# Linear attention with a top-2 MoE FFN on one core: TensorE takes the tile loop in source order instead of the planner's

## The chip, the cores and the metric

The kernel runs on one core of a Trainium2 chip. The metric is the device time of that core in microseconds (us), as the median of several runs.

## The reference

The input x has 8 sequences of 1024 tokens with 256 features, all in float32. In short:

```python
xn = layernorm(x)
# linear attention, 16 heads of 16
q, k, v = xn @ Wq.T, xn @ Wk.T, xn @ Wv.T
q, k = elu(q) + 1, elu(k) + 1
kv = cumsum over tokens of (k outer v)        # per head, causal
den = clip(q . cumsum(k), 1e-6)
att = (q . kv / den) @ Wo.T
# mixture of experts: 8 experts, two per token
logits = xn @ Wr + br
weights, experts = top_k(logits, 2); weights = softmax(weights)
y_e = (silu(xn @ W1[e]) * (xn @ W3[e])) @ W2[e]     # 256 -> 512 -> 256
out = x + att + sum over the token's two experts of weight * y_e
```

## The kernel before

**Tiling.** The 8192 tokens are cut into 16 blocks of 512 (`NBLK`); a block has 4 chunks of 128. The MoE part works on tiles of 128 rows that belong to one expert. The rows of a tile are gathered by an indirect DMA, and its weights are fetched by expert number. 132 such tiles are run by the loop, and up to three more behind it under a condition. The first 25 tiles come from a first list that covers the first 2048 tokens only, so that the loop can begin while the other 12 blocks are still to be normalised and routed. The other tiles come from a second list over the rest.

**Prelude.** The first four blocks are normalised and routed, and the first list is built, in an order written by hand (`tc.manual_schedule` for VectorE, ScalarE, TensorE and GpSimd). It is not changed.

**The tile loop** is `for j in range(NM + 1)`. One iteration holds, in the source, these parts:

- `ffn_norm(j + 1)` (ScalarE) normalises the gathered rows of the next tile. Up to tile 26 they are transposed on TensorE (`ffn_turn`, tile `xg_t`); from tile 27 on by a DMA on 16-bit halves (`ffn_halves`, `ffn_turn_halves`, joined by `ffn_join`).
- For j = 1 to 11 one token block t = 4 + j is prepared. `moments` works out mean and variance of two blocks at once on VectorE (at even j): for each of 8 chunks a `bn_stats` and a `bn_aggr` (L282, L283), then a reciprocal square root by Newton steps. `normalise(t)` is four ScalarE activations (L317). `turn(t)` is eight transposes on TensorE (L332, tile `tp`) with a ScalarE copy for each half (`xnT`, L337). `logits` is eight matmuls of 32 columns (L355), copied to `lgT`, turned once more (`lg_t`, L376) and added to `lg_all` on VectorE by `add_logits`. After every fourth block `route` picks the two experts on VectorE; its first part runs up to some counts, and the rest, driven by exhausting the generator `routing`, begins with the count matmuls on TensorE (`cnt_ps`, L442 and L448, read at L453).
- At j = 12 (`LISTS`) `second_batch` begins to build the second list, and one `next(lists)` per tile for j = 12 to 21 drives it. It has 32 groups of four matmuls (`held_ps`, L724) of one-hot matrices that VectorE makes for each group (`at_place` L572, `held` L585, `parts` L590); ScalarE makes the other half of `parts` with four multiplications (L592). In between, VectorE counts other tokens and works out `fills`.
- For j = 12 to 23 a DMA copies a piece of x into the output.
- `attend_upto(n)` moves the attention on. It has 9 steps a block: projections to q, k and v (`zq` L794; `zkk`, `zkv` L810; eight matmuls each), transposes, denominators, and one step for each chunk. A chunk's step issues on TensorE: `attend` of the chunk before it (`a_ps`, L990, 2 matmuls with `oT`), `carry` (`o_ps<-qT,kv`, L930), `scores` of the next chunk (`s_ps`, L911, eight matmuls of 32 rows), `weigh` (`o_ps<-s_sb`, L948, 16 matmuls of 32 columns, and L958, eight for the new `kv`). VectorE applies four causal masks to the scores (`s_sb`, L918), and makes `oT` (L965) and `kv` (L968, L977).
- `ffn_step(j)` starts the DMAs of later tiles and issues `ffn_hidden(j)`: gate and up, eight matmuls each (`gu_ps`, L1265), ScalarE's silu (L1273) and VectorE's product (`hT`, L1276). Then come `ffn_turn` or `ffn_join` of tile j + 1, and `ffn_out(j - 1)`: four matmuls (`y_ps`, L1284), scaled on VectorE (`y`, L1291), added to the output by an indirect DMA (L1295).

**What sets the order.** In the loop a planner orders the instructions of every engine; it reads the source as a list with dependencies and takes from what is ready by its own estimates. Only instructions inside `in_order(...)` keep the source's order among themselves. Each engine then takes its own list strictly in order. So the order on TensorE before is not that of the source: the transposes and logits of a block, for example, lie between single matmuls of the attention or of gate and up. When two attention steps fall into one iteration (this happens seven times from tile 26 on), the second step's `a_ps`, `carry` and `weigh` come between gate and up of the following tile.

**Buffers in PSUM.** `ps_mm` has four buffers (`gu_ps`, `s_ps`, `zq` and `zk`, `zv`), `ps_y` two (`y_ps`, `a_ps`, `lg_ps`, `lg_t`, `cnt_ps`, `held_ps`, the denominators), `ps_t` two (`tp`, `xg_t`, `o_ps`). A matmul waits until its buffer's last reader, on VectorE or ScalarE, is done.

Of the kernel before, what the change touches and what calls it, by code (L numbers as in the profile page):

```python
# [46 lines left out]
F32 = mybir.dt.float32  # L47
# [7 lines left out]
P = 128  # L55
# [9 lines left out]
def tile_attention_moe(  # L65
# [257 lines left out]
    def turn(t):  # L323
        xn = scaled.pop(t)
        if 0 < t < FB:
            xnT = e_one.tile([P, KC, TB], F32, name=f"xnT{t}")
        else:
            xnT = (two if t == 0 else f_two).tile([P, KC, TB], F32, tag="xnT", name="xnT")
        for k in range(KC):
            tp = ps_t.tile([P, TB], F32, tag="t", name="tp")  # L330
            for c in range(NCH):
                done = nc.tensor.transpose(  # L332
                    tp[:, bass.ts(c, P)], xn[:, c, bass.ts(k, P)], ident
                )
                if t == FB + 1:
                    in_order(done)
            nc.scalar.copy(xnT[:, k, :], tp)  # L337
        turned[t] = xnT
        if t == 0:
            turned_first.append(xnT)  # L340
        elif t != FB - 1:
            store(t)
# [352 lines left out]
    def second_batch(taken):  # L695

        rows = sizes(True)
        left = f_one.tile([P, E], F32, name="left")
        nc.vector.tensor_tensor(left, rows, taken, ALU.subtract)
        upto = add_up(left, "upto2")  # L700
        past = past_experts(upto, N2, f_x, "xb")
        te, te_i = numbers_of(past, N2, "2")
        nc.vector.tensor_copy(rows_left, upto[0:1, E - 1 : E])

        room = f_one.tile([P, E - 1], F32, name="room2")
        nc.vector.tensor_scalar(
            room, rows[:, 0 : E - 1], -1.0, float(ROWS), ALU.mult, ALU.add
        )
        nc.vector.tensor_tensor(room, room, taken[:, 1:E], ALU.add)
        of_tiles = rows_of(past, past, room, taken[:, 0:1], N2, "rows2")  # L710
        in_row, place = places(NT)

        short = f_one.tile([P, E], F32, name="short")
        nc.vector.tensor_scalar(short, rows, 1.5, None, ALU.is_lt)
        num_i = const.tile([P, N2], I32, name="of2_i")
        all_held = f_one.tile([P, N2], F32, name="all_held")
        yield
        for j in range(2):
            for a in range(0, NT, 16):
                ps = ps_y.tile([P, 2, N2], F32, tag="y", name="held_ps")  # L720
                for b in range(a, a + 16, PART):
                    at, parts = one_hot(in_row, place, of_tiles, j, b, N2)
                    for i in range(PART):
                        nc.tensor.matmul(  # L724
                            ps.rearrange("p w n -> p (w n)"), lhsT=at[:, i, :],
                            rhs=parts[:, i].rearrange("p w n -> p (w n)"),
                            start=(b + i == a), stop=(b + i == a + 15),
                        )
                for w in range(2):
                    if j == 0 and a == 0 and w == 0:  # L730
                        nc.vector.tensor_copy(all_held, ps[:, 0, :])
                    else:
                        nc.vector.tensor_tensor(all_held, ps[:, w, :], all_held, ALU.add)
                if j == 0 and a == 16:
                    fill = other_tokens(short)
                    fills = f_one.tile([P, N2], F32, name="fills")
                    for e in range(E):
                        mine = fills
                        if e > 0:
                            mine = f_two.tile([P, N2], F32, tag="mine", name="mine")  # L740
                        nc.vector.tensor_scalar(
                            mine, te, float(e), fill[:, e : e + 1], ALU.is_equal, ALU.mult
                        )
                        if e > 0:
                            nc.vector.tensor_tensor(fills, fills, mine, ALU.add)
                yield
        nc.vector.tensor_copy(num_i, all_held)
        _, src_i = tokens(all_held, N2, NT, "2_i")
        empty = f_one.tile([P, N2], F32, tag="at_i", name="empty")
        nc.vector.tensor_scalar(empty, all_held, 0.5, None, ALU.is_lt)  # L750
        nc.vector.tensor_tensor(empty, empty, fills, ALU.mult)
        dst_i = const.tile([P, N2], I32, name="dst2_i")
        nc.vector.tensor_tensor(dst_i, src_i, empty, ALU.add)
        batches[1] = tab_d[1], te_i, num_i, src_i, out_rows, dst_i
        yield
# [495 lines left out]
            if s == 0 and halved and j >= TURNED:  # L1251
                ffn_turn_halves(j)

    def ffn_hidden(j, last=False):


        gu = []
        for s in range(2):
            if last and s == 1:
                ffn_out(j - 1, True)  # L1260
            w13 = ws.pop((j, s))
            ps = ps_mm.tile([P, IC, P], F32, tag="mm", name="gu_ps")
            for i in range(IC):
                for k in range(KC):
                    done = nc.tensor.matmul(  # L1265
                        ps[:, i, :], lhsT=w13[:, k, bass.ts(i, P)], rhs=xgT[j][:, k, :],
                        start=(k == 0), stop=(k == KC - 1),
                    )
                    if last:
                        in_order(done)  # L1270
            gu.append(ps)
        hT = ffn2.tile([P, IC, P], F32, tag="hT", name="hT")
        silu = nc.scalar.activation(hT, gu[0], AF.Silu)  # L1273
        if j == 0:
            in_order(silu)
        nc.vector.tensor_tensor(hT, gu[1], hT, ALU.mult)  # L1276
        hs[j] = hT
# [22 lines left out]

    stored = [0]

    def ffn_step(j, behind):


        while loaded[0] < min(NM, j + (5 if j >= READ else 4)):
            ffn_load(loaded[0])
            loaded[0] += 1
        if j + 2 < NM:
            ffn_weights(j + 2)  # L1310
        if j < NM:
            ffn_hidden(j, j == NM - 1)
        if j + 1 < TURNED:
            ffn_turn(j + 1)
        elif j + 1 < NM:
            ffn_join(j + 1)
        if j > 0 and j != NM - 1:
            ffn_out(j - 1)
        for _ in range(2):
            if stored[0] < j - behind:  # L1320
                ffn_store(stored[0])
                stored[0] += 1
# [15 lines left out]
    LISTS = NBLK - FB  # L1338
    READ = LISTS + 10
    AHEAD = 2 + LISTS // 2 + 3 * (READ - LISTS) // 2  # L1340
    for j in range(NM + 1):
        if j + 1 < TURNED:
            ffn_norm(j + 1)
        if TURNED <= j + 2 < NM:
            ffn_norm(j + 2)
            ffn_halves(j + 2)
        t = FB + j
        counting = FB < t <= NBLK and t % ROUND == 0
        if counting and t == NBLK:
            for _ in routing:  # L1350
                pass
        if 0 < j and t < NBLK:
            if j % 2 == 0:
                with tc.issue_after((last_token if j < 4 else last_masked)[0].ins):
                    for _ in moments(t, 2):
                        pass
            normalise(t)
            turn(t)
            if t + 5 < NBLK:
                load_x(t + 5, nc.scalar)  # L1360
            add_logits(t, 1, logits_turned(t))
            if (t + 1) % ROUND == 0:
                routing = route(t + 1 - ROUND, t + 1)
                next(routing)
        if j == LISTS:
            in_order(
                nc.sync.dma_start(
# [2 lines left out]
                )  # L1370
            )
            in_order(nc.sync.dma_start(out=tab_d[1][0:1, :], in_=before[0:1, 0:3]))
            lists = second_batch(taken)
        if LISTS <= j < READ:
            next(lists)
        if LISTS <= j < LISTS + NBLK - FB:
            t = FB + j - LISTS
            rows = slice(t * TB, (t + 1) * TB)
            in_order(nc.sync.dma_start(out=out_rows[rows, :], in_=x_rows[rows, :]))
        if j < LISTS:  # L1380
            attend_upto(3 + j // 2)
        elif j < READ:
            attend_upto(AHEAD - 3 * (READ - j - 1) // 2)
        else:
            attend_upto(AHEAD + (LAST - 1 - AHEAD) * (j - READ + 1) // (NM - 1 - READ) + j // (NM - 1))
        ffn_step(j, LATE if N1 < j <= N1 + LATE else 0)
        if counting and j < LISTS:
            for _ in routing:
                pass
        if j == N1 + 1:  # L1390
            copied.append(j)
            in_order(nc.sync.dma_start(out=out_rows[0 : FT * P, :], in_=acc_d[:, :]))
    assert steps_made[0] == LAST
    while stored[0] < NM:
        ffn_store(stored[0])
# [51 lines left out]
```

## Time and profile before

| what | value |
|---|---|
| runs | 1267.0, 1267.89, 1276.63 us; median 1267.89 us |
| profiled execution, its own time | 1267.09 us |
| its span, first to last instruction | 1265.3 us |
| TensorE busy (matmuls) | 1217.8 us (96%) |
| TensorE weight loads | 1057.0 us (84%), beside the matmuls |
| VectorE busy | 676.0 us (53%) |
| ScalarE busy | 557.1 us (44%) |
| GpSimd busy | 519.9 us (41%) |
| mean granted TensorE clock | 0.991 |
| first matmul starts, last one ends | 10.9 us, 1250.4 us |
| gate of tile 1, 12, 26 starts | 59.7, 172.7, 337.9 us |

Busy time is the time in which an engine carried out instructions; weight loads of TensorE run beside its matmuls and are listed apart. The granted clock is the share of the full TensorE clock that the chip allowed. In the trace's lists, `L1265 PE MATMUL gu_ps<-xgT,w` is a matmul from line 1265 that writes tile `gu_ps` from `xgT` and `w`; a float32 matmul leaves two records, so the 16 matmuls of gate and up appear as x32.

### The profile page before, as it was taken

Reading aid. Unit: us, or ns where it says so; the run is one execution under the profiler, and the core shown is the slowest. Engines: PE = TensorE matmul, PEld = TensorE weight load, DVE = VectorE, ACT = ScalarE, POOL = GpSimd, SP = SyncE. Lnnn points to the kernel's source line nnn. Section 1 sums busy time; section 2 is a strip of 40 time slices with the busy share of each in tenths; the row PEclk is TensorE's granted clock in tenths of the full one; section 3 lists DMA queues with packets and bytes.
Section 4 is the critical chain, followed back from the end, with each engine's and each line's share of the span. In section 5 each row is a group of like instructions: output and inputs, shape, how many; then the busy total and the mean of one; then the engine's idle time right before and its main releaser. Section 6 shows DMA issues by size and latency. Waiting matters only on the chain.

```text
span 1265.3 us, 29694 instructions
## 1 busy us (share of the span) xinstructions
PE 1217.8 (96%) x11434; PEld 1057.0 (84%) x11434; DVE 676.0 (53%) x1541; ACT 557.1 (44%) x1062; POOL 519.9 (41%) x460
## 2 busy tenths in 40 slices
PE   5899999999999999999999999999999999999995
PEld 3577887787898998888888889989888889899884
DVE  7767589863354454545454544545453544545451
ACT  4565465461433526262623426162625344262620
POOL 3643233233344544443435444443544444443422
PEclk9999999999999999999999999999999999999997
DMA  9897565557788697969789897979897787969782
GB/s 329 289 288 242 168 189 119 187 155 208 206 201 194 165 235 164 225 173 211 168 194 203 164 234 155 223 181 192 185 206 171 198 202 170 216 154 231 167 176 35
DMA packets 203678, 245.84 MB, mean 194 GB/s; under 512 B 72674, under 2 KB 127586, under 8 KB 203250
## 3 DMA queue, kind: packets, MB, share of 16 engines
q1 hardware_dynamic: 160146, 189.65, 52.2%
q0 software_dynamic: 38064, 43.27, 24.5%
q10 hardware_dynamic: 5328, 11.01, 2.4%
q8 instruction: 94, 1.54, 0.5%
q14 instruction: 46, 0.38, 0.1%
HBM read 187.91 MB, written 44.29 MB: 184 GB/s over the span
## 4 chain that ended last, share of the span: by engine, by line
PE 86%; DVE 6%; DMA 3%; ACT 2%; issue 1%; POOL 1%; SPq 0%; POOLq 0%; DVEq 0%; ACTq 0%
PE gu_ps L1265 36%; PE y_ps L1284 16%; PE s_ps L911 6%; PE o_ps L948 5%; PE a_ps L990 4%; PE zq L794 4%; PE zkv L810 4%; PE zkk L810 4%; PE o_ps L930 2%; PE tp L332 1%; PE tp L857 1%; DMA halfT<-half 1%; PE lg_ps L355 1%; DVE at_place L572 1%; PE den L879 1%
## 5 line engine op out<-in xcount | busy, mean ns | idle before, releaser
L1265 PE MATMUL gu_ps<-xgT,w 128*128 128x128 f32 x4224 | 507.8, 278 | 1.2 <-DVE s_sb L918 0.8
L1265 PEld LDWEIGHTS gu_ps<-xgT,w 128*128 128x128 f32 x4224 | 488.0, 192 | 19.9 <-issue 13.5
L1295 POOL DMA_INDIRECT out_dram<-y,dst_i x107 | 175.5, 1640 | 338.4 <-DVE y L1291 72.9
L1284 PE MATMUL y_ps<-w_sb,hT 128*128 x1056 | 250.9, 381 | 1.8 <-DVE hT L1276 1.6
L1175 POOL DMA_INDIRECT xg<-in_x_dram,src_i x132 | 128.3, 972 | 230.5 <-DVE half L1198 99.0
L1284 PEld LDWEIGHTS y_ps<-w_sb,hT 128*128 128x128 f32 x1056 | 190.9, 191 | 23.2 <-DVE hT L1276 2.0
L918 DVE TENSOR_TENSOR s_sb<-s_ps,causal 128x512 f32<-128x512 f32 x256 | 159.9, 683 | 86.8 <-PE s_ps L911 76.8
L1273 ACT ACTIVATE hT<-gu_ps 128x512 f32<-128x512 f32 x132 | 78.8, 597 | 284.5 <-PE gu_ps L1265 279.8
L1276 DVE TENSOR_TENSOR hT<-gu_ps,hT 128x512 f32<-128x512 f32 x132 | 90.4, 685 | 64.9 <-PE gu_ps L1265 36.6
L1180 POOL DMA_INDIRECT entry<-tab_d,of_i x107 | 105.9, 990 | 42.3 <-issue 31.7
L1198 DVE COPY half<-xg 128x512 uint16<-128x512 uint16 x105 | 47.9, 457 | 132.4 <-ACT xg L1188 132.4
L1291 DVE TENSOR_SCALAR y<-y_ps,entry 128x256 f32<-128x256 f32 x132 | 63.7, 483 | 101.5 <-PE y_ps L1284 101.4
L995 ACT COPY at<-a_ps 128x256 f32<-128x256 f32 x64 | 23.7, 371 | 169.5 <-PE a_ps L990 127.0
L911 PE MATMUL s_ps<-qm,kT 32*128 32x256 f32 x1024 | 89.0, 405 | 1.7 <-DVE hT L1276 1.6
L1216 ACT COPY xgT<-halfT 128x512 uint16<-128x512 uint16 x105 | 79.7, 760 | 4.9 <-DMA halfT<-half 4.8
L1188 ACT ACTIVATE xg<-xg,entry 128x256 f32<-128x256 f32 x132 | 78.8, 598 | 3.6 <-DMA entry<-tab_d,num_i 3.6
L990 PE MATMUL a_ps<-wo_sb,oT 128*128 128x256 f32 x256 | 68.4, 389 | 3.0 <-DVE oT L965 2.8
L948 PE MATMUL o_ps<-s_sb,va 128*32 128x128 f32 x2048 | 70.7, 278 | 0.0
L911 PEld LDWEIGHTS s_ps<-qm,kT 32*128 32x128 f32 x1024 | 51.8, 184 | 20.9 <-issue 10.7
L948 PEld LDWEIGHTS o_ps<-s_sb,va 128*32 128x32 f32 x2048 | 52.8, 110 | 18.1 <-issue 15.5
L1295 POOL DMA_INDIRECT acc_d<-y,src_i x25 | 41.2, 1649 | 53.1 <-DVE y L1291 18.0
L794 PE MATMUL zq<-xnT,wq_sb 128*128 128x512 f32 x128 | 60.3, 613 | 0.3 <-DVE s_sb L918 0.3
(215 smaller groups left out, 1343.9 us busy)
## 6 DMA issues: line engine op xcount, KB each, us to landing
w<-in_w_dram SPq DMA_DIRECT2D x264, 512.0 KB
rden<-over SPq DMA_DIRECT2D x128, 64.0 KB
xnT_d<-xnT ACTq DMA_DIRECT2D x15, 512.0 KB
xnT<-xnT_d SPq DMA_DIRECT2D x15, 512.0 KB
out_dram<-at POOLq DMA_DIRECT2D x13, 512.0 KB
out_dram<-in_x_dram SPq DMA_DIRECT2D x12, 512.0 KB
xb<-in_x_dram SPq DMA_DIRECT2D x10, 512.0 KB
w_sb<-in_w_dram SPq DMA_DIRECT2D x4, 1024.0 KB
```

Source lines behind the costliest of these rows:

```text
L794: nc.tensor.matmul(z, lhsT=wq_sb[:, k, bass.ts(o, P)], rhs=xnTs[t][:, k, :], start=(k == 0), stop=(k == KC - 1),)
L810: nc.tensor.matmul(z[:, i, :], lhsT=xnTs[t][:, k, bass.ts(c + i, P)], rhs=wkv_sb[:, k, a, :], start=(k == 0), stop=(k == KC - 1),)
L911: nc.tensor.matmul(s_ps[r][:, hh].rearrange("p a l -> p (a l)"), lhsT=kT[rows, hh, span], rhs=qm[rows, hh, :, span], start=True, stop=True,)
L918: last_masked[0] = nc.vector.tensor_tensor(sm, s_ps[r].rearrange("p k a l -> p (k a) l"), causal_b, ALU.mult)
L948: nc.tensor.matmul(o_ps[32 * r : 32 * r + 32, hh, :], lhsT=va[:, c, 4 * hh + r, a, :], rhs=s_sb[r][:, 2 * hh + a, :], start=(first and a = ...
L990: nc.tensor.matmul(a_ps, lhsT=oT[:, hh, :], rhs=wo_sb[:, hh, :], start=(hh == 0), stop=(hh == 1),)
L1175: rows = nc.gpsimd.indirect_dma_start(out=xg[j], out_offset=None, in_=x_rows[:, :], in_offset=bass.IndirectOffsetOnAxis(ap=src_i[:, i : i ...
L1180: nc.gpsimd.indirect_dma_start(out=entry[j], out_offset=None, in_=table[:, :], in_offset=bass.IndirectOffsetOnAxis(ap=num_i[:, i : i + 1], ...
L1265: done = nc.tensor.matmul(ps[:, i, :], lhsT=w13[:, k, bass.ts(i, P)], rhs=xgT[j][:, k, :], start=(k == 0), stop=(k == KC - 1),)
L1276: nc.vector.tensor_tensor(hT, gu[1], hT, ALU.mult)
L1284: done = nc.tensor.matmul(y_ps, lhsT=hT[:, i, :], rhs=w2_sb[:, bass.ds(e * (IC * H) + i * H, H)], start=(i == 0), stop=(i == IC - 1),)
L1295: nc.gpsimd.indirect_dma_start(out=rows[:, :], out_offset=bass.IndirectOffsetOnAxis(ap=dst_i[:, i : i + 1], axis=0), in_=ys.pop(j), in_off ...
```

## The change

TensorE's order in the tile loop is no longer left to the planner: the loop body becomes `tile_step(j)`, called under `tc.manual_schedule(engines={EN.PE})`, so that TensorE takes its instructions in the order of the source. The other engines stay with the planner. The source order is rearranged with it:

- A block is normalised one iteration earlier than it is turned: `normalise(t + 1)`, and `moments` at odd j for the blocks t + 1 and t + 2.
- The order in an iteration is now attention, `turn(t)`, gate, `logits(t)`, up, then (at j = 4, 8 and 12) the rest of routing with the counts, `xg_t` or the join of the next tile, `lg_t` with `add_logits` and the start of `route`, and y of the tile before.
- `second_batch` yields before each group of four matmuls. It begins at the end of iteration 12, and five `piece()` calls in each of the iterations 13 to 20 move it on: at the start, behind the attention, between gate and up, behind up, and at the end.
- The copies of x into the output are issued ahead of the attention.

```diff
@@ turn
-                done = nc.tensor.transpose(
+                nc.tensor.transpose(
                     tp[:, bass.ts(c, P)], xn[:, c, bass.ts(k, P)], ident
                 )
-                if t == FB + 1:
-                    in_order(done)
@@ second_batch
                     at, parts = one_hot(in_row, place, of_tiles, j, b, N2)
+                    yield
                     for i in range(PART):
@@ ffn_hidden(j, last=False, between=None)
+            if between and s == 1:
+                between()
@@ ffn_step(j, behind, between, after, late)
-            ffn_hidden(j, j == NM - 1)
+            ffn_hidden(j, j == NM - 1, between)
+            after()
         if j + 1 < TURNED:
             ffn_turn(j + 1)
         elif j + 1 < NM:
             ffn_join(j + 1)
+        late()
         if j > 0 and j != NM - 1:
             ffn_out(j - 1)
@@ the loop
-    for j in range(NM + 1):
+    held = {}
+
+    def tile_step(j):
+        nonlocal routing
...
+        turning = 0 < j and t < NBLK
         counting = FB < t <= NBLK and t % ROUND == 0
-        if counting and t == NBLK:
-            for _ in routing:
-                pass
-        if 0 < j and t < NBLK:
-            if j % 2 == 0:
-                with tc.issue_after((last_token if j < 4 else last_masked)[0].ins):
-                    for _ in moments(t, 2):
+        pieces = LISTS < j < READ - 1
+
+        def piece():
+            if pieces:
+                next(held["lists"])
+
+        def between():
+            if turning:
+                held["lgT"] = f_two.tile([P, P], F32, tag="lgT", name="lgT")
+                logits(t, held["lgT"])
+            piece()
+
+        def after():
+            if counting:
+                for _ in routing:
+                    pass
+            piece()
+
+        def late():
+            nonlocal routing
+            if turning:
+                tp = ps_y.tile([P, P], F32, tag="y", name="lg_t")
+                nc.tensor.transpose(tp, held.pop("lgT"), ident)
+                add_logits(t, 1, tp)
+                if (t + 1) % ROUND == 0:
+                    routing = route(t + 1 - ROUND, t + 1)
+                    next(routing)
+
+        if t + 1 < NBLK:
+            if j % 2:
+                with tc.issue_after((last_token if j < 3 else last_masked)[0].ins):
+                    for _ in moments(t + 1, 2):
                         pass
-            normalise(t)
+            normalise(t + 1)
+        if LISTS <= j < LISTS + NBLK - FB:
+            rows = slice((t - LISTS) * TB, (t - LISTS + 1) * TB)
+            in_order(nc.sync.dma_start(out=out_rows[rows, :], in_=x_rows[rows, :]))
+        piece()
...
+        piece()
+        if turning:
             turn(t)
             if t + 5 < NBLK:
                 load_x(t + 5, nc.scalar)
-            add_logits(t, 1, logits_turned(t))
-            if (t + 1) % ROUND == 0:
-                routing = route(t + 1 - ROUND, t + 1)
-                next(routing)
+        ffn_step(j, LATE if N1 < j <= N1 + LATE else 0, between, after, late)
+        piece()
         if j == LISTS:
...
-            lists = second_batch(taken)
-        if LISTS <= j < READ:
-            next(lists)
...
-        if counting and j < LISTS:
-            for _ in routing:
-                pass
+            held["lists"] = second_batch(taken)
+            next(held["lists"])
+        if j == READ - 2:
+            next(held["lists"])
...
+    with tc.manual_schedule(engines={EN.PE}):
+        for j in range(NM + 1):
+            tile_step(j)
```

## Prediction, made before the changed kernel was run

> **What bounds the kernel now.** I read the page's busy times first, then the chain that ended last.
>
> ```profile
> PE 1217.8 (96%) x11434; PEld 1057.0 (84%) x11434; DVE 676.0 (53%) x1541; ACT 557.1 (44%) x1062; POOL 519.9 (41%) x460
> ...
> PE 86%; DVE 6%; DMA 3%; ACT 2%; issue 1%; POOL 1%; SPq 0%; POOLq 0%; DVEq 0%; ACTq 0%
> ```
>
> TensorE (PE) is busy for 96% of the 1265.3 us and is 86% of the chain. Time can come only from shorter or fewer PE gaps and a better packing of its matmuls, and it is lost wherever PE must now wait. The averages hide where, so I took the windows by stage: tiles 1 to 11, tiles 12 to 25, tile 26 to the last matmul (columns: window, length, then PE, weight load, VectorE, ScalarE, GpSimd busy, granted clock, DMA share, GB/s).
>
> ```profile
> 59.70:172.70 113.00, 111.04 (x1053) 89.61 (x1052) 73.68 (x288) 59.32 (x119) 43.43 (x38) 1.00 0.76 229
> 172.70:337.90 165.20, 156.43 (x1404) 129.64 (x1403) 113.41 (x258) 79.83 (x224) 56.14 (x46) 0.99 0.60 168
> 337.90:1250.40 912.50, 910.43 (x8685) 810.01 (x8683) 442.52 (x815) 385.68 (x652) 387.32 (x318) 1.00 0.84 190
> ```
>
> In the third stage PE idles 2.1 us of 912.5 and VectorE has half its time free. In the first two PE idles 1.96 and 8.8 us, and VectorE is two thirds busy. DMA is no bound: weights land 10 us or more before their matmuls from tile 3 on.
>
> Next, the timeline of PE in one undisturbed tile (start, length, instruction). PE starts each run of matmuls before the one before it has ended, so I price a run from its start to the next start.
>
> ```profile
> 599.72 1.89 PE L1284 MATMUL y_ps<-w_sb,hT 128*128 x8
> 601.45 1.03 PE L990 MATMUL a_ps<-wo_sb,oT 128*128 128x256 f32 x4
> 602.31 0.61 PE L930 MATMUL o_ps<-qT,kv 128*128 128x128 f32 x4
> 602.85 1.15 PE L911 MATMUL s_ps<-qm,kT 32*128 32x256 f32 x16
> 603.92 1.08 PE L948 MATMUL o_ps<-s_sb,va 128*32 128x128 f32 x32
> 604.82 0.31 PE L958 MATMUL o_ps<-va,kn 128*32 128x32 f32 x16
> 605.06 3.84 PE L1265 MATMUL gu_ps<-xgT,w 128*128 128x128 f32 x32
> 608.73 1.89 PE L1284 MATMUL y_ps<-w_sb,hT 128*128 x8
> ```
>
> So: y 1.73, a_ps 0.86, carry 0.54, scores 1.07, weigh 0.90, its kv 0.24, gate and up 3.57 together (3.67 here with the change of array shape). In the same way elsewhere: a projection 3.43 to 3.55, eight transposes of a block 0.87, a block's logits 0.57, xg_t 0.22, lg_t 0.11, four one-hot matmuls 0.39. Going between whole-array and 32-row or 32-column matmuls costs about 0.1 each way, which is why the planner's mixing in the first stage is dear:
>
> ```profile
> 83.55 0.69 PE L911 MATMUL s_ps<-qm,kT 32*128 32x256 f32 x2
> 84.17 0.44 PE L332 MATMUL tp<-ident,xb 128*128 128x128 f32 x2
> 84.54 0.69 PE L911 MATMUL s_ps<-qm,kT 32*128 32x256 f32 x2
> 85.17 0.66 PE L332 MATMUL tp<-ident,xb 128*128 128x128 f32 x4
> ```
>
> A lone scores matmul takes 0.62 from start to start; eight together take 1.07.
>
> **The change part by part.** PE issues the same matmuls; only their order changes, from the planner's to the source's. VectorE, ScalarE and GpSimd stay with the planner and keep their work (two table loads of ScalarE fewer).
>
> *Packing.* I wrote down PE's new order tile by tile and summed the prices. Tile 3, for instance: gate and up 3.57, logits 0.57, xg_t 0.22, lg_t 0.11, y 1.73, scores 1.07, transposes 0.87, three changes of shape 0.31: 8.45. Tiles 1 to 11 come to 97.2 against 113.0 now (-15.8), tiles 12 to 25 to 143.7 against 165.2 (-21.5). From tile 26 on PE's order is the old one but for seven places.
>
> *Waits in tiles 1 to 11.* The planner's mixing covered them; a fixed order queues everything behind a waiting matmul, the next gate and up above all. Each is "input ready" minus "PE there", from old durations. Logits in tiles 3, 6 and 7 need the second xnT copy (ScalarE, 584 ns), which stands behind four activations of 592 ns for the block ahead, and these behind the moments on VectorE (eight times 400 + 165 ns and the Newton steps): about 2.0, 0.9 and 0.9. The gate of tile 4 needs a PSUM buffer freed by a mask that stands behind some 14 routing operations of about 290 ns: 2.6. y in tiles 4 and 8 gets its buffer from add_logits, again behind moments: 2.1 and 3.1. The second half of the transposes waits for a ScalarE copy in tiles 5, 7 and 9: 1.1, 0.9, 0.9. Together 14.5; bounds 0 (VectorE ahead everywhere) and 20 (each wait half as long again).
>
> *Waits in tiles 12 to 25.* The second list starts from routing's last counts. Now:
>
> ```profile
> 168.05 0.29 DVE L453 TENSOR_TENSOR pos<-cnt_ps,count 128x128 f32<-128x128 f32 x1 [0.23 <-PE cnt_ps L448]
> ...
> 180.56 0.56 PE L724 MATMUL held_ps<-parts,at_place 128*128 128x220 bf16 x4
> ```
>
> From the counts to the first one-hot matmul it is 12.5 us, filled with other matmuls. After the change the counts come behind up in tile 12, 4.2 us into it, so the first one-hot can start at 16.7, while PE has done all that stands ahead of it at 9.4: a wait of 7.3. In tiles 13 to 20 one-hot groups stand at four fixed places a tile; each needs VectorE first:
>
> ```profile
> L572 DVE TENSOR_TENSOR at_place<-cols,place 128x512 bf16<-128x512 f32 x32 | 21.9, 684 | 2.7 <-PE held_ps L724 2.7
> L585 DVE TENSOR_TENSOR held<-rows,in_row 128x440 bf16<-128x440 f32 x32 | 19.0, 609 | 1.1 <-ACT parts L592 0.9
> L590 DVE TENSOR_SCALAR parts<-held,row 128x440 bf16<-128x440 bf16 x32 | 10.7, 335 | 0.0
> ```
>
> 1.63 us a group, 6.5 a tile, beside hT, y, masks and a block's sums. Tile 14 (scans of 1.25 each, the fills, the reciprocal) asks 18.8 us of VectorE against 12.9 of PE: 5.5 of wait, with 1.0 in tile 13. Tiles 15 to 25 add 7.9: 2.75 in 18 and 19 (ScalarE loads a table twice, 1.28 each), 2.65 in 17, 2.5 in the rest. Together 21.7; bounds 8 (only the list's start, which the order makes certain) and 32 (half as long again).
>
> *Seven double steps.* Where two attention steps fall into one tile, the planner now puts the second between gate and up. The new order puts its a_ps straight behind the first's kv matmuls, but a_ps needs oT:
>
> ```profile
> 396.62 1.08 PE L948 MATMUL o_ps<-s_sb,va 128*32 128x128 f32 x32
> 396.70 2.49 DVE L918 TENSOR_TENSOR s_sb<-s_ps,causal 128x512 f32<-128x512 f32 x4 [1.88 <-PE s_ps L911]
> 397.51 0.31 PE L958 MATMUL o_ps<-va,kn 128*32 128x32 f32 x16
> 397.75 2.05 PE L1265 MATMUL gu_ps<-xgT,w 128*128 128x128 f32 x16
> 399.11 0.41 DVE L965 TENSOR_TENSOR oT<-rden,o_ps 128x256 f32<-128x256 f32 x1
> 399.64 1.06 PE L990 MATMUL a_ps<-wo_sb,oT 128*128 128x256 f32 x4
> ```
>
> VectorE takes the four masks first, so oT ends at 399.52, 1.77 behind the matmul that follows kv (397.75). It is hidden now by gate's 1.79. After, with the 0.1 from its end to the next matmul, PE waits 1.85, seven times: +13.0. In the new order VectorE still has masks, oT, kv. Carry's own input is ready 2.56 behind, less than 1.85 + 0.86, and adds nothing. Bounds 10 and 15.
>
> *The clock.* Two profile rows show that a short PE gap can cost more than itself: a_ps waited 1.29 us, and the clock granted next was a half for 3.41 us.
>
> ```profile
> 306.25 1.25 PE L990 MATMUL a_ps<-wo_sb,oT 128*128 128x256 f32 x4 [1.29 <-DVE oT L965]
> ...
> 307.13:310.54 3.41, 3.41 (x55) 2.91 (x54) 0.29 (x1) 0.37 (x1) 0.00 (x0) 0.50 0.32 69
> ```
>
> That loses 1.7 us. Three other gaps of 0.7 to 1.2 us brought none. I take half of the seven waits of 1.85 and a third of the six waits of 2 us or more ahead of them: (3.5 + 2) x 1.7 = 9; bounds 0 and 20 (twelve dips).
>
> The Trainium skill ("TensorE: Matmul & The Clock Gate", section "Why this matters for your kernels") says that only an idle gap over about 3 us between bursts drops the clock. By it only the 7.3 us wait and the 5.5 in tile 14 would, making the term 3 and the time 1282; the row above, a drop behind a gap of 1.29 us, speaks against leaving the shorter waits out, and the sum does not use the rule.
>
> **Sum.** -15.8 - 21.5 + 14.5 + 21.7 + 13.0 + 9 = +20.9: span 1286.2. The profiled run took 1267.09, 1.8 around its span and 0.8 under the median of 1267.89, so 1288.
>
> **The rivals** follow from W, the early waits and dips together, 45.2 above; the rest is -24.3.
> - Waits half as long. VectorE is a third idle in these stages, and the planner may order it to suit the known PE order. W of 25: 1268; up to W = 37, 1280. It speaks against it that routing, moments and one-hots are chains, not throughput. 0.30.
> - Faster. VectorE and ScalarE stay ahead, since blocks are normalised a tile earlier and their inputs are in place when PE comes; then the packing gain of 37.3 in tiles 1 to 25 stays and only the double steps' 13.0 is paid: span 1241, time 1243. It decides once W is below 11.6, yet the list's start alone asks 7.3. 0.10.
> - The list is late. Should VectorE's load in tiles 13 to 16 (it was busy 46.8 of 49.1 us where the one-hots began) push every group back, waits rise to their upper bounds and most places dip: W = 20 + 32 + 15 = 67, time 1310. 0.10.
> - The order does not take effect: 1268; the instruction order shows that it does. 0.
>
> **How the numbers follow.** The forecast, 1288, has 0.50 (its own range 1281 to 1304). About 1% (12.7 us: 1255.2 to 1280.6) is what a measurement of this kernel tells from no change. Slower: 0.50 + 0.10; within: 0.30; faster: 0.10. The range 1260 to 1306 leaves out the fast case and part of the late list.
>
> **What would show it.** Right: tiles 1 to 25 about as long as now (278 us) with PE's busy time some 30 us smaller and its idle larger; a_ps waiting 1.8 for oT at seven places; a gap of several us ahead of the first held_ps; more slices with half clock. Wrong: tiles 1 to 25 under 255 us, no a_ps waits, or a third stage that differs at more than seven places.

## Result and the profile after

The changed kernel takes 1272.31 us (median of 20 runs) beside 1268.44 us before (20 runs): a ratio of 1.0031 (95% interval 1.0019 to 1.0042), measurably slower, but by a fifth of what was forecast. The profiled execution took 1272.98 us, with a span of 1271.2 (before 1267.09 and 1265.3), so the two traces differ by 5.9 us.

The same three stages in the windows of the profile after (window, length, then TensorE, weight load, VectorE, ScalarE, GpSimd busy, granted clock, DMA share, GB/s):

```profile
59.81:169.21 109.40, 101.38 (x1047) 87.69 (x1046) 68.42 (x267) 58.90 (x119) 42.96 (x37) 0.99 0.77 232
169.22:333.12 163.90, 150.30 (x1410) 130.15 (x1409) 118.77 (x276) 76.25 (x222) 57.15 (x46) 0.98 0.61 171
333.13:1258.36 925.23, 911.38 (x8685) 809.21 (x8683) 440.76 (x815) 386.53 (x652) 388.12 (x319) 1.00 0.82 187
```

Tiles 1 to 11 are 3.6 us shorter (113.0 before), tiles 12 to 25 1.3 shorter (165.2), and the rest is 12.7 longer (912.5). TensorE's busy time falls by 9.7 and 6.1 us in the first two stages, which is the better packing, and most of it turns into waiting. In the third it is busy as before and idle 13.9 us instead of 2.1. The waits of TensorE in that stage (engine, tile, line, what it waited for: us in all, times, longest) name one cause:

```profile
PE a_ps L989 <- DVE oT L964: 12.2, 7, 1.7
PE y_ps L1285 <- DVE hT L1277: 0.9, 1, 0.9
PE s_ps L910 <- DVE hT L1277: 0.8, 2, 0.5
```

One of the seven places, in the timeline (start, length, instruction; idle time before it in brackets):

```profile
391.13 1.08 PE L947 MATMUL o_ps<-s_sb,va 128*32 128x128 f32 x32
391.22 2.48 DVE L917 TENSOR_TENSOR s_sb<-s_ps,causal 128x512 f32<-128x512 f32 x4 [1.88 <-PE s_ps L910]
392.03 0.31 PE L957 MATMUL o_ps<-va,kn 128*32 128x32 f32 x16
393.62 0.41 DVE L964 TENSOR_TENSOR oT<-rden,o_ps 128x256 f32<-128x256 f32 x1
...
394.08 1.13 PE L989 MATMUL a_ps<-wo_sb,oT 128*128 128x256 f32 x4 [1.75 <-DVE oT L964]
```

VectorE takes the four masks first, oT ends at 394.03, and a_ps, now straight behind the kv matmuls, waits 1.75 us with everything behind it. Before, the first half of the next tile's gate and up lay in between.

The long wait of tile 12 is there too, VectorE's chain from the counts to the first one-hot:

```profile
173.59 0.29 DVE L451 TENSOR_TENSOR pos<-cnt_ps,count 128x128 f32<-128x128 f32 x1 [1.08 <-PE cnt_ps L446]
...
184.99 0.91 PE L723 MATMUL held_ps<-parts,at_place 128*128 128x220 bf16 x4 [5.99 <-DVE parts L588]
```

### The profile page after: what moved, and what is told of

Its sections match the earlier page's. It is cut to its first block, busy times and chain, and to the rows that moved or that the text cites. A ratio compares the mean times of both kernels' runs of the same rounds, so it can differ in the third digit from the quotient of the medians.

```text
span 1271.2 us, 29689 instructions
## 1 busy us (share of the span) xinstructions
PE 1203.9 (95%) x11434; PEld 1055.2 (83%) x11434; DVE 674.9 (53%) x1541; ACT 554.3 (44%) x1060; POOL 521.8 (41%) x460
## 5 line engine op out<-in xcount | busy, mean ns | idle before, releaser
L989 PE MATMUL a_ps<-wo_sb,oT 128*128 128x256 f32 x256 | 68.4, 390 | 16.4 <-DVE oT L964 14.9
L910 PE MATMUL s_ps<-qm,kT 32*128 32x256 f32 x1024 | 76.0, 401 | 0.8 <-DVE hT L1277 0.8
L989 PEld LDWEIGHTS a_ps<-wo_sb,oT 128*128 128x128 f32 x256 | 46.5, 189 | 28.4 <-DVE oT L964 16.2
L809 PE MATMUL zkv<-wkv_sb,xnT 128*128 128x256 f32 x256 | 61.2, 394 | 0.0
```

Source lines behind the costliest of these rows:

```text
L989: nc.tensor.matmul(a_ps, lhsT=oT[:, hh, :], rhs=wo_sb[:, hh, :], start=(hh == 0), stop=(hh == 1),)
```

## Experiments

The kernels of experiments 1 to 4 and 6, the first pair of 7 and the third run of 8 ran in sessions in which the kernel before took 1269 to 1270 us, the others in sessions in which it took 1290 to 1292. So ratios to the kernel before of the same session are compared. The expectations speak of chips, but the chip numbered 0 on record shows both levels, so what differs is not known. In brackets stands the 95% interval of a ratio.

**1. The double steps divided.** In the changed kernel the second attention step of the seven iterations goes between gate and up of the next tile, as the planner had it:

```diff
         def between():
...
+            if j >= READ and steps_made[0] % STEPS == STEPS - 1:
+                attend_upto(due(j))
...
-            attend_upto(AHEAD + ...)
+        attend_upto(due(j), hold=j >= READ)   # stops short of step 8 if it is the second
```

> The changed kernel, but at the seven places from tile 26 on where two attention steps fall into one iteration, the second step (a_ps, carry, weigh) is issued between gate and up of the next tile instead of straight behind the first; nothing else moves on TensorE. Theory: the 12.7 us that the stage from tile 26 on grew by are the seven waits of a_ps for oT, and nothing else there; then the time is 1272.3 - 12.7 = 1259.6 (1258 to 1262), below the kernel before by what tiles 0 to 25 and the end gained. Rival: the wait is only moved, since silu and hT of the tile then come late behind the masks and y waits for hT: 1266 to 1272.

Measured: 1263.84 us, ratio 0.9954 (0.9935 to 0.9974). The stage from tile 26 on:

```profile
335.30:1246.90 911.60, 910.63 (x8685) 809.34 (x8683) 441.65 (x815) 385.92 (x652) 389.00 (x319) 1.00 0.84 190
```

911.6 instead of 925.2, and no wait of a_ps is left: the theory holds for that stage, the rival falls. The time lies between their two bands: the whole gained some 10 us, not 12.7, because tile 26 begins 2.2 us later (335.3 against 333.1) and the end became longer. From TensorE's last matmul to the end of the span it takes 15.2 us here, 14.9 before and 12.9 in the changed kernel; the last two stores of rows go through GpSimd's queue behind the last piece of attention output, and that piece is later when the last double step is divided.

**2. Counts and list start ahead of gate in iteration 12.**

```diff
+        if j == LISTS:
+            for _ in routing:
+                pass
+            ... the table's DMAs, second_batch, its first next() ...
         if turning:
             turn(t)
```

> The changed kernel, but routing's last counts and the beginning of the second list are issued ahead of gate in iteration 12, not behind up and at the end of it. Theory: the 6.0 us idle ahead of the first held_ps matmul is the chain from the counts to the first one-hot matrix, which now starts some 4.2 us earlier; the gap shrinks to about 1.8 and the time to 1268 (1266 to 1270). Rival: VectorE is the limit through tiles 13 to 16, so what tile 12 gains comes back as waits of held_ps in tiles 13 and 14: 1271 to 1273.

Measured: 1268.2 us, 0.9991 (0.9974 to 1.0009), so some 5 us below the changed kernel's ratio. The gap is as expected:

```profile
180.53 0.55 PE L723 MATMUL held_ps<-parts,at_place 128*128 128x220 bf16 x4 [1.85 <-DVE parts L588]
```

Tile 12 goes from 16.4 to 11.5 us, and tiles 13 to 16 do not give it back (48.2 us against 49.9). The rival, VectorE as the limit there, falls. Two stretches of half clock that the changed kernel has in tiles 12 to 14 (at 184.4 and 204.9 us) do not occur here, so part of the gain is clock.

**3. The planner on the new source.** `tc.manual_schedule` is taken off the loop.

> The changed kernel's source, but TensorE in the loop is ordered by the planner again. Theory: the rearranged source alone brings the packing in tiles 1 to 11 (the planner's list now holds transposes, logits and scores mostly in whole groups), and the planner keeps the double steps apart and lets other matmuls go ahead of those that wait; without the seven waits (12.7) and with shorter early waits it takes 1253 to 1260. Rival: the gain in tiles 1 to 25 comes from the fixed order itself; left to the planner, the one-hot groups are scattered again and the early tiles are as long as before the change: 1266 to 1270.

Measured: 1263.93 us, 0.9953 (0.9935 to 0.997), above the theory's band and below the rival's. By stage:

```profile
59.30:165.30 106.00, 103.33 (x1048) 89.52 (x1047) 67.78 (x268) 58.70 (x119) 43.15 (x37) 0.99 0.80 241
165.30:332.10 166.80, 155.56 (x1409) 130.93 (x1408) 116.95 (x276) 76.82 (x222) 62.48 (x46) 0.98 0.59 166
332.10:1244.90 912.80, 911.17 (x8685) 809.45 (x8683) 441.92 (x815) 385.84 (x652) 386.98 (x318) 1.00 0.84 190
```

Tile 26 begins at 332.1, with the fixed order at 333.1. What tiles 1 to 25 gained therefore comes from the rearranged source, which the planner can use as well; as it stands in the changed kernel, the fixed order adds nothing there and costs the seven waits later (experiment 5 changes this). Within the first stages the two trade: the planner is 3.4 us better in tiles 1 to 11 and 2.9 worse in 12 to 25, where it scatters the one-hot groups (tile 19 takes 17.2 us instead of 8.0).

**4. Logits straight behind the transposes.**

```diff
             turn(t)
+            held["lgT"] = f_two.tile([P, P], F32, tag="lgT", name="lgT")
+            logits(t, held["lgT"])
```

> The changed kernel, but the logits of a block are issued straight behind its transposes, not between gate and up of the tile. Theory: the first half of the logits can run at once, the second waits for the second xnT copy on ScalarE (584 ns, behind the first), so each of eleven tiles gets a wait of 0.6 to 1.0 in place of the one of 0.5 to 0.9 that only tiles 3 and 7 have: 1272.3 + 6 to 9 = 1278 to 1281. Rival: the copy is early enough and only the packing counts (one change of matmul shape less or more): 1271 to 1274.

Measured: 1289.85 us in only four runs (1283 to 1296), 1.0168 (1.0135 to 1.0201); the profiled execution took 1283.08, 10.1 more than the changed kernel's. Its groups of instructions in tiles 1 to 11 (line, engine, operation, tiles, shapes, count, then busy us, mean ns, idle before and its releaser), and those of the changed kernel below:

```profile
L353 PE MATMUL lg_ps<-xnT,wr_sb 128*32 128x128 f32 x164 | 9.2, 295 | 7.8 <-ACT xnT L335 7.3
```

```profile
L353 PE MATMUL lg_ps<-xnT,wr_sb 128*32 128x128 f32 x176 | 7.5, 280 | 1.4 <-ACT xnT L335 1.4
```

The wait for the copy grows by 5.9 us, and tiles 0 to 11 by 8.5 (126.1 against 117.6). So the place between gate and up is worth what the theory said; why the timed runs lost more than the profiled one is open.

**5. Both edits together** (1 and 2, and the double step of tile 17 divided too), and the planner with edit 2.

> The changed kernel with both edits of the first two experiments: double attention steps divided around gate (the one of tile 17 too), counts and list start ahead of gate in iteration 12. Theory: the two act in different stages, so the gains add: the divided steps took it to 1263.8, the counts brought 4 to 5, tile 17 its 1.8 of wait: 1258 (1255 to 1261). Rival: VectorE is the limit behind tile 12 and the divided step of tile 17 only moves the wait to the one-hots: 1262 to 1264.

> The changed kernel's source with the planner ordering TensorE, and the counts and list start ahead of gate in iteration 12. Theory: as with the fixed order the first one-hot comes some 4 us earlier and the list ends earlier; 1263.9 - 4 = 1260 (1257 to 1262), level with the fixed order with both edits. Rival: the planner already fills the wait in tile 12 with the transposes of k, so nothing is to be had there: 1263 to 1265.

Measured: with both edits 0.991 (0.9879 to 0.994; 1277.05 us beside 1292.24), which is the theory's ratio. The planner with edit 2: 0.9997 (0.9965 to 1.0029), no better than the 0.9953 without it in the other session; the rival is nearer, and nothing was gained there. These two ran in one session, and their intervals do not meet: with both edits the fixed order is about 1% faster than the planner on the same source with edit 2. Repeated later beside 1289.67 us, again a slower session:

> The changed kernel with both edits once more (0.991 of the kernel before on a chip on which that took 1292). On a chip on which the kernel before takes 1268 to 1270: theory, the two edits act in different stages and add up, 0.9955 of the divided steps alone less 0.004 for the counts: 0.991 (0.989 to 0.994). Rival, the slow chip flattered it: 0.995.

Measured: 0.9903 (0.9871 to 0.9934). The gains add, and only the same kernel without normalising ahead (experiment 7) stands level with it. A run of this very kernel in a session where the kernel before takes 1268 to 1270 us is missing, so the rival of this repetition is not excluded; the variant of experiment 6 ran in such a session and stood at 0.9924.

**6. The attention ended three iterations earlier**, on top of both edits, to shorten the end:

```diff
-  (LAST - 1 - AHEAD) * (j - READ + 1) // (NM - 1 - READ) + j // (NM - 1)
+  (LAST - 1 - AHEAD) * (j - READ + 1) // (NM - 4 - READ) + j // (NM - 4)
```

> The run with both edits, and the attention's last steps are due three iterations earlier, so that the last piece of attention output (at, added to the output in DRAM by GpSimd's queue) is issued some 25 us before the end. Theory: the 12.8 to 15.2 us between TensorE's last matmul and the end of the span are GpSimd's chain of adding DMAs (4.4 us each, at among them); without at in it the end comes 4.4 us earlier, 0.0035 below the ratio with both edits (0.991): 0.987 to 0.988. Rival: the chain is set by the last two row stores alone, which start behind the last y: same ratio, 0.991.

Measured: 1261.96 us, 0.9924 (0.99 to 0.9947). The theory's ratio lies outside, the rival's inside. TensorE ends at 1240.2, but the span at 1260.7, 20.5 us later, since the row stores stand in a chain of their own:

```profile
1244.16 1.56 POOL L1296 DMA_INDIRECT out_dram<-y,dst_i  x1 [4.81 <-issue]
1248.74 1.56 POOL L1296 DMA_INDIRECT out_dram<-y,dst_i  x1 [3.02 <-DMA out_dram<-y,dst_i]
1253.28 1.55 POOL L1296 DMA_INDIRECT out_dram<-y,dst_i  x1 [2.98 <-DMA out_dram<-y,dst_i]
```

One store starts 4.5 us behind another, each waiting for the landing of the one before. The rival reckoned with two stores, and here three are left; why the first of them starts only at 1244.16 the trace does not show. TensorE does not set the very end of this kernel.

**7. Normalising in the same iteration again** (moments at even j, `normalise(t)`), beside the changed kernel itself.

> The changed kernel itself, unedited, beside the other three on this chip, since the chip of the last four runs took longer for the kernel before too (1292). On a chip like the first: 1.003 of the kernel before. If slow transfers are what that chip differs by, the ratio may be lower than 1 there, as the run with both edits stood at 0.991 and the divided steps alone at 0.995 on the first chip.

> The changed kernel, but a block is again normalised in the iteration in which it is turned (moments at even j for the blocks t and t + 1). Theory: the transposes then wait for the four activations of 592 ns and, at even j, for the moments ahead of them, in most of eleven tiles: +15 to 25 us. Rival: the planner orders VectorE and ScalarE anyway and pulls the moments and activations ahead of the iteration, as it did in the kernel before, so that only ScalarE's order changes: 0 to +4 us.

Measured: the changed kernel 1.0046 (1.0029 to 1.0063), without normalising ahead 1.0006 (0.9992 to 1.0021). The theory fell: VectorE and ScalarE are ordered by the planner and do the work early anyway. The two intervals do not meet, so in these runs normalising ahead even cost 0.4%. Whether it does was tried once more on top of both edits:

> The changed kernel with both edits, and blocks normalised in the iteration in which they are turned. If normalising ahead costs the 0.4% that the two ratios differ by, 0.987; if the equal profiles tell the truth, the same as without this edit, 0.991 within 0.002.

Measured: 0.9897 (0.9868 to 0.9927), the same as without (0.9903). The spans of the profiled pair in the first comparison, 1271.3 and 1271.5, are equal too. So this part of the change brings nothing, and the cost of 0.4% was not seen a second time.

**8. What length of gap drops the clock.** At the seven double steps more VectorE work is put on oT, its value unchanged:

```diff
         nc.vector.tensor_tensor(oT, rden[:, c], o_ps, ALU.mult)
+        if twice[0] and t > 2:
+            for _ in range(4):          # 10, 1, 4 and 2 in the other runs
+                nc.vector.tensor_scalar(oT, oT, 1.0, None, ALU.mult)
```

> The changed kernel with four more multiplications by one on oT at each of the seven double steps from tile 26 on, so that a_ps waits there some 1.2 to 1.5 us longer than 1.85 (oT's value is the same). It measures what length of wait drops the clock. Prediction's view (half of all waits near 2 us do): four or more half-clock windows behind the seven places, time 1272 + 7 x 1.4 + 7 = 1289. Rival (a wait this short drops it rarely; the changed kernel's seven places showed none): 0 or 1 such window, 1280 to 1283.

> As the run before, with ten multiplications: waits of some 5 us. If a stretch of 3.41 us must be without any matmul, and the stretches run freely, about (5 - 3.4) / 3.4, half of the seven waits, are followed by half clock, and part of that window lies in the wait itself: time 1272 + 7 x 3.5 + 3 x 1 = 1300. If any busy share below some half is enough, all seven are: 1308.

> The changed kernel with one more multiplication by one on oT at the seven double steps from tile 26 on, for waits of some 2.5 us. At 1.75 us of idle time in front of a_ps none of the seven places was followed by half clock in the changed kernel, at 3.7 us seven of seven were. If it takes an idle time of a certain length, these seven go one way together; if it is a matter of where the wait lies in a running window, some of them go and some do not.

> The changed kernel with four more multiplications by one on oT at the seven double steps, as in the first of these runs, beside a shorter wait on the same chip. If the length of the gap decides, six or seven of the seven places (3.25 to 3.7 us) are followed by half clock; if it was the chip, none or one.

> The same with two multiplications, for gaps of 2.7 to 2.9 us, between the lengths tried so far. If a gap must fill a stretch of some 3 us, none of the seven; if the chance grows evenly with the length from 2.4 to 3.3, about half.

Single runs: 1326.49, 1342.96 (kernel before 1292.24), 1279.16 (1270.18), 1317.22 and 1305.82 (1289.67). Counted at the seven places in all profiles that have the waits, a gap of TensorE and whether a stretch of half clock began in it or within 4.5 us behind it (in the first run six of the seven gaps were followed, where the third expectation says seven):

| gap in front of a_ps, us | half clock followed |
|---|---|
| 1.6 to 1.75 (five kernels with unlengthened waits) | 2 of 35 |
| 2.28 to 2.45 | 0 of 7 |
| 2.62 to 2.82 | 3 of 6 |
| 3.25 to 3.79 | 14 of 15 |
| 5.22 to 5.54 | 7 of 7 |

The last two runs shared a session, and half of the gaps of 2.62 to 2.82 went another way than those of 3.29 to 3.79 there, so the session does not decide it. Nor does the length alone: a_ps waits the same 1.75 us at tile 17, which the table leaves out, and there 4 of the 7 profiles that have this wait show half clock behind it.

What decides is how the gap lies. In each of the 18 profiles every stretch of half clock begins on one grid, whose steps are 3.413 us long, and lasts one or more whole steps (the last, behind TensorE's last matmul, aside). Here are two gaps of the first run on this grid (columns as in the first table of windows; length less TensorE's busy time is its idle time):

```profile
1063.19:1066.60 3.41, 1.82 (x57) 1.28 (x52) 2.90 (x6) 0.00 (x0) 1.08 (x2) 1.00 1.03 118
1066.60:1070.02 3.42, 1.63 (x12) 1.41 (x16) 1.66 (x7) 0.37 (x1) 2.47 (x2) 1.00 0.36 41
...
1216.79:1220.20 3.41, 0.62 (x3) 0.57 (x4) 2.67 (x8) 0.00 (x0) 2.80 (x3) 1.00 0.58 81
1220.20:1223.62 3.42, 3.42 (x43) 2.89 (x45) 0.00 (x0) 0.37 (x1) 1.69 (x2) 0.50 0.18 44
```

The gap of 3.25 us lies across two steps, which are idle for 1.59 and 1.79 us, and the clock stays whole, in the step behind them too. Of the gap of 3.58 us, 2.79 lie in one step, and the next step has half clock. Counted from tile 1 to the last matmul in all 18 profiles, over the steps that have the whole clock themselves:

| idle time of TensorE in one step, us | next step at half clock |
|---|---|
| under 1.2 | 0 of 6092 |
| 1.2 to 2.0 | 25 of 120 |
| over 2.0 | 38 of 38 |

This is a count over the traces, not a test that was set up for it, but it explains the odd rows of the table above: the seven gaps of 2.28 to 2.45 us all lay across two steps, with at most 1.77 in one. What decides between 1.2 and 2.0 us stays open. The Trainium skill ("TensorE: Matmul & The Clock Gate", section "Why this matters for your kernels") puts the limit at gaps over some 3 us. These runs differ: three gaps of 2.62 to 2.82 us were followed by half clock and one of 3.25 was not. The times of the first two runs lie above both expectations, by more than the 24 us by which the kernel before was slower in their session; the unedited changed kernel was not run beside them, so no cost of half clock is read from them.

## Why the prediction was wrong

The direction was right and the time far too long: 20.9 us were forecast in the span, 5.9 came. (On the median of 1267.89 the sum gives 1288.8; the prediction writes 1288.) Point by point, from the profiled executions:

| term | forecast | measured |
|---|---|---|
| tiles 1 to 11, packing and waits | -15.8 + 14.5 = -1.3 | -3.6 |
| tiles 12 to 25, packing and waits | -21.5 + 21.7 = +0.2 | -1.3 |
| seven double steps | +13.0 | +12.7 |
| the clock | +9 | no row of its own: some 3, within the rows above |
| ahead of tile 1 | 0 | +0.1 |
| from TensorE's last matmul to the end | 0 | -2.0 |

**The waits in tiles 1 to 25** are the step that failed most: 14.5 + 21.7 = 36.2 us were forecast, and TensorE idles 8.0 + 13.6 = 21.6 us there. The forecast took each as "input ready" minus "PE there", with the inputs' old durations and places in VectorE's and ScalarE's queues. Nearly all the waits it names are in the profile, but smaller (the logits' wait is the last line of experiment 4):

```profile
PE y_ps L1285 <- DVE lg_all L364: 2.6, 2, 1.5
PE tp L332 <- ACT xnT L335: 2.0, 3, 0.7
PE gu_ps L1266 <- DVE s_sb L917: 1.7, 1, 1.7
```

| wait, us | forecast | idle time measured |
|---|---|---|
| y for add_logits (tiles 4 and 8) | 5.2 | 2.6 |
| transposes for the xnT copy | 2.9 | 2.0 |
| gate of tile 4 for a mask | 2.6 | 1.7 |
| logits for the xnT copy | 3.8 | 1.4 |
| the list's start | 7.3 | 6.0 |
| tiles 13 and 14 | 6.5 | 2.0 |
| tiles 15 to 25 | 7.9 | 5.6 |

So the inputs came earlier than the old places say. Experiment 7 points the same way: where the source puts the work of normalising did not set when it was done. Which instruction came earlier at each wait was not followed up.

**The clock** is the second step that failed. Of its 9 us, 3 were for a third of six early waits, and this came: half clock at 184.4 and 204.9 us, behind the waits in tiles 12 and 14, cost some 3 us (half of two steps of 3.41) and is part of the row for tiles 12 to 25, as the one at 307.1 was before. The other 6 were for half of the seven waits of 1.85 us, and none of them came; over five kernels it was 2 of 35. The rate was made out of one row. The gap of 1.29 us in it left 1.41 us idle in one step of the grid, where 25 of 120 steps are followed by half clock, not half of them. The profile before also had six other gaps of 0.67 to 1.22 us without a drop, not the three that the prediction counts. The rule that it set aside was not the answer either: applied to the waits that came, it gives the drop in tile 12, but not that in tile 14, where two gaps of 0.64 and 0.83 us fell into one step, and its forecast, 1282, would still have been too long by 10.

**The double steps** were right to 0.3 us, in mechanism (masks ahead of oT, a_ps behind kv), in number and in size; experiment 1 removed them and got the old stage length back.

**Packing** fell short the other way and hid part of this. Tiles 1 to 25 take 273.3 us; less the 21.6 idle and the 3 for half clock, 248.7 are left, where 97.2 + 143.7 = 240.9 were forecast: of the gain of 37.3 us some 29.5 came. TensorE's busy time fell by 15.8 us, and the prediction looked for some 30. Part of the difference of 7.8 belongs to the 21 waits, since a wait costs more than its idle time (the gate of tile 4 idles 1.66 us and starts 1.88 later than the prices say); how much was not worked out. So it is luck that the two early stages came as near to the forecast as the table shows.

**The end** was missing in the sum. The forecast let everything follow TensorE's last matmul at the old distance. That distance goes with the place of the last double step: 11.9 to 12.9 us in all kernels that have it in one piece, 14.9 to 18.1 in those that have it divided around gate, and 20.5 in experiment 6, which tried to shorten it. The link is read from the traces alone.

**The rivals.** The case that came true is the first, early waits and dips smaller than reckoned: 109.4 - 97.2 = 12.2 and 163.9 - 143.7 = 20.2, together 32.4 instead of 45.2, for which its sum gives 1276; the end's 2.0 does most of the rest. It had a chance of 0.30. Its reason, that the planner orders VectorE to suit, fits the smaller waits, but its total also holds the packing that did not come. That VectorE and ScalarE run ahead altogether, and that the list is late, did not happen.

## What to carry to other kernels

A fixed order on one engine pays only once the waits that it uncovers are taken out. As first written it gained nothing over the planner on the same source, which had the same gain in tiles 1 to 25, and it lost the planner's cover at seven places; with the double steps divided and the list begun earlier it was about 1% faster than the planner, in the one session in which both ran. When a step is written directly behind its producer's last matmul, follow the reader through the other engine's queue (here four masks ahead of oT), and put the work of that length in between by hand. Do not make a rate out of one row: look for all places of the same kind in the trace, and count those in which nothing happened.

## What the hardware showed

- In these 18 profiles the clock goes by TensorE's idle time in fixed steps of 3.413 us, not by the length of a gap: over 2.0 us idle in one step, the next was at half clock (38 of 38); under 1.2 us it never was (0 of 6092). A gap of 3.25 us that lay across two steps passed without a drop; two gaps of 0.64 and 0.83 us that fell into one step, in the changed kernel's profile, were followed by one.
- Row stores that add into the same DRAM tensor, each of which waits here for the landing of the one before, start 4.5 us apart, and three of them stretched the end to 20.5 us behind TensorE's last matmul.
- The same kernel took 1268 to 1270 us in some sessions and 1290 to 1292 in others. In the slower sessions iteration 0 took 13.8 to 16.1 us instead of 7.4 to 9.5 for every arrangement profiled there; what else differs is not shown.
